# Four pieces of the next rows' preparation at earlier points of VectorE's order, and one tile for the last three row stores

## The chip, the cores and the metric

The kernel runs on one core of a Trainium2 chip. The metric is the device time of one launch in microseconds (us), the median of several runs. TensorE, VectorE, ScalarE and GpSimd each work through a queue of instructions in order; SyncE (SP) issues most of the DMAs. Semaphores tie the queues together. In the profile they are PE, DVE, ACT, POOL and SP.

## The reference

x has 8 rows (batch entries) of 512 tokens with 256 features. All is in float32. What is computed, with the shapes that matter:

```python
nx = layer_norm(x) * ln_gamma + ln_beta                    # (8, 512, 256)
k, v = context @ Wk, context @ Wv                          # context (8, 64, 256)
weights = softmax(nx @ Wq @ k.T / 16)                      # (8, 512, 64)
evidence = weights @ v
combined = concat([nx, evidence, anchor])                  # 768 features, anchor is cond of the row
router = softmax(combined @ router_W + router_b)           # 3 experts
h = silu(combined @ e_w1[e] + e_b1[e])                     # (8, 512, 512) for each expert
routed = sum_e router[e] * (h @ e_w2[e] + e_b2[e])
g = sigmoid(silu(combined @ gate_w1 + gate_b1) @ gate_w2 + gate_b2)
out = x + g * (routed @ out_w + out_b)
```

## The kernel before

**Tiling.** Two rows of x are handled together: a loop runs over four row pairs, j = 0 to 3. For each, `gate_layer` makes the hidden layer of the gate, `expert_layer` is called for the experts e = 0, 1, 2, and `outputs` makes the gate, the experts' second layer and the stores. Products of two rows are combined in a scheme with seven products in place of eight, so that each hidden chunk is put together from several PSUM parts. `keep_part` (L830) is a copy on ScalarE that takes a part out of PSUM and thereby lets TensorE go on in that bank, `add` (L827) is an addition on VectorE, `silu` (L821) is on ScalarE. `weigh` (L868, L872) multiplies hidden chunks by the router's probabilities, on VectorE, from a list that is worked off in order at several points. In `outputs`, `subtract` (L1063) forms differences of hidden chunks ahead of the products that read them, L1073 starts a sum with the biases, and `keep` (L1079) adds to it from PSUM.

**Order.** Every queue's order is the order of the Python calls; no scheduler changes it. The preparation of the next row pair is spread over the work of this one: a dictionary names steps for points such as (1, "B"), point B in the layer of expert 1, and `run` calls the steps of a point in the order in which they were put. Points in a layer are, in order, W, A, B, C and D. Work that belongs to the weights, which are turned and combined while the first row pair runs, is put in the same way and ahead of the next rows' steps. Two of its parts matter here: `transpose_second` (L486, VectorE) turns a block of second-layer weights into the tile scr_w2T, and `second_layer` (L494) multiplies it on TensorE and copies it out on ScalarE (L499). `combine_second` (L233 to L236) then works on GpSimd.

**Preparation of the next pair.** Its steps, with their engines:

- `load_x` (L146, SP) loads the two tiles of x, b0 and b1.
- `statistics` (L540, L541, VectorE) finds mean and variance, four pairs of instructions for a tile.
- `deviation` (L544, ScalarE) takes the square root of the variances. The square root and the silu belong to different function tables of ScalarE.
- `normalize` (L549, L552, VectorE) is one reciprocal and four multiplications in place.
- `store_x` (L600, SP) stores the normalized tile to scratch memory, four DMAs a tile, and `regroup_x` (L468, SP) loads it again in another order, eight DMAs.
- `router_part` (L590, VectorE) multiplies the normalized x by a vector and sums along x, four instructions a tile, each with a second one that reads the sum; `logits` in it has a small memset (L581) on GpSimd.
- `transpose_blocks` (L612, VectorE, then L563 on ScalarE) turns what was regrouped.

`load_x_blocks` (L468, SP) loads this pair's x once more for the final addition (tile xb, read by L1096 on GpSimd).

**The end.** The last pair ends in `outputs` with products by tokens: `token_experts` gives three PSUM tiles, and `finish_rows` (L1179 to L1181) multiplies and adds on VectorE and stores. Its output tile has the tag yb, of which there are two buffers; the tile y_tokens before it has the same tag.

Of the kernel before, what the change touches and what calls it, by code (L numbers as in the profile page):

```python
# [8 lines left out]
F32 = mybir.dt.float32  # L9
# [7 lines left out]
def kernel(  # L17
# [51 lines left out]
    nc = tc.nc  # L69
    P = 128  # L70
    B, T, H = x.shape
# [3 lines left out]
    NT = T // P  # L75
# [15 lines left out]
    work = ctx.enter_context(tc.tile_pool(name="work", bufs=2))  # L91
# [439 lines left out]
    S = {}  # L531
# [376 lines left out]
    def finish_groups(j, groups):  # L908

        for n in groups:  # L910
            silu(j, n, 0, 1, U[n])
            if n:
                add(n, 1, 0, Z[n])
# [5 lines left out]
    def expert_layer(j, e, steps):  # L919
        a, b = PAIRS[e]  # L920

        def run(point):
            for step in steps.get((e, point), ()):
                step()

        if e:
            finish_groups(j, PAIRS[e - 1])
        for i in range(2):
            S["h", i, e] = h_tile(i, e, f"h_{2 * j + i}_{e}")
        U[a] = bank(3, f"ps_u_{j}_{a}")  # L930
        nx_product(j, a, 1, True)
        keep_part(a, 0, 0, U[a])
        if not e:
            nx_product(j, 0, 4)
        U[b] = bank(1, f"ps_u_{j}_{b}")
        nx_product(j, b, 1, True)
        if not e:
            finish_groups(j, (0,))
        keep_part(b, 0, 0, U[b])
        finish_odd(j, PAIRS[e - 1] if e else (0,))  # L940
        if not e:
            silu(j, 0, 1, 1)
        if e > 1 or e and j:
            weigh(j, 4)
            run("W")
            weigh(j, 1)
        spares(*Z_BANKS[1 - e % 2])
        nx_product(j, a, 2)
        add(a, 0, 0, Y[a])
        nx_product(j, a, 5)  # L950
        keep_part(a, 1, 1, Z[a])
        run("A")
        nx_product(j, a, 6)
        keep_part(a, 1, 0, U[a])
        silu(j, a, 0, 0)
        nx_product(j, b, 6)
        keep_part(b, 1, 0, U[b])
        nx_product(j, b, 2)
        add(b, 0, 0, Y[b])
        nx_product(j, b, 5)  # L960
        keep_part(b, 1, 1, Z[b])
        silu(j, b, 0, 0)
        spares(*Z_BANKS[1 - e % 2], 4, 6)
        run("B")
        for n in (a, b):
            nx_product(j, n, 7)
            add(n, 1, 1, U[n])
        for n in (a, b):
            weigh_early(n)
        run("C")  # L970
        if e:
            weigh(j, 6 if j or e > 1 else 10)
        for n in (a, b):
            silu(j, n, 1, 1)
            weigh_rest(n)
        for n in (a, b):
            nx_product(j, n, 3)
        run("D")
        for n in (a, b):
            nx_product(j, n, 4)  # L980
        if e + 1 < E:
            fresh(j, e + 1)
            evidence(j, [(m, False) for m in (a, b)] + [(m, True) for m in PAIRS[e + 1]])
        else:
            evidence(j, [(m, False) for m in (a, b)])
# [13 lines left out]
    def outputs(j, steps):  # L999
# [22 lines left out]
        u, z, y = (bank(i, f"ps_g{n}_{j}") for n, i in (("u", 0), ("z", 2), ("y", 4)))  # L1022
# [89 lines left out]
        def finish_late(r, ps, i, row):  # L1112
            g = gated(ps, i, row, slice(0, T))
            nc.vector.tensor_tensor(r, r, g, ALU.add)
            nc.vector.transpose(g, r)
            store(g, i, row, slice(0, T), (nc.scalar, nc.sync))
# [57 lines left out]
            for q in range(NQ):  # L1174
                product(ps, hidden(j, q, 1, 0)[:, t * P : (t + 1) * P], a(q, 0, 1), start=q == 0)

        def finish_rows(rest, ps, t, queue):
            y = work.tile([P, P], F32, tag="yb", name=f"y_rows_{t}")
            nc.vector.tensor_tensor(y, ps, rest[:, 0, t - 1, :], ALU.mult)  # L1179
            nc.vector.tensor_tensor(y, y, rest[:, 1, t - 1, :], ALU.add)  # L1180
            queue.dma_start(out[2 * j, t * P : (t + 1) * P, :P], y)  # L1181
# [14 lines left out]
        for t in range(1, NT):  # L1196
            token_experts(tokens[t - 1], t)
        finish_late(r21, u, 1, 0)
        for t in range(1, NT):
            finish_rows(rest, tokens[t - 1], t, nc.scalar if t % 2 else nc.sync)  # L1200


    with tc.manual_schedule(engines=None):
# [62 lines left out]
        for j in range(NP):  # L1266


            within, between = {}, {}

            def put(where, n, step, *args):
                where.setdefault(n, []).append(lambda: step(*args))

            if j == 0:
                put(within, "gate", value_weights, 0, 1)
                put(within, (0, "A"), anchor_rows, 1)
                put(within, (0, "A"), router_logits, 0)
                put(within, (0, "A"), load_second, 1)
                put(within, (0, "B"), second_bias)
                put(within, (0, "C"), transpose_second, 0)  # L1280
                put(within, (0, "C"), anchor_columns, 1)
                put(within, (0, "C"), anchor_rows, 2)
                put(within, (0, "C"), router_exp, 0)
                put(within, (0, "D"), router, 0)
                put(within, (0, "C"), load_second, 2)
                put(within, (0, "D"), second_layer, 0)
                put(within, (0, "D"), spread_probabilities, 0)
                put(within, (0, "D"), combine_second, 0)
                put(within, (1, "A"), transpose_second, 1)
                put(within, (1, "B"), second_layer, 1)  # L1290
                put(within, (1, "B"), combine_second, 1)
                put(within, (1, "C"), transpose_second, 2)
                put(within, (1, "C"), anchor_columns, 2)
                put(within, (1, "D"), second_layer, 2)
                put(within, (1, "D"), combine_second, 2)
            if j:
                put(within, "gate end", spread_probabilities, j)
            if j and j + 1 < NP:
                put(within, (0, "B"), statistics, 2 * j + 3, 0, NT)
            put(within, (0, "C" if j == 0 else "B"), value_weights, j, 2)  # L1300
            put(within, (1, "C"), load_x_blocks, 2 * j)
            put(within, (2, "A"), gate_differences, j)
            put(within, (2, "C"), load_x_blocks, 2 * j + 1)
            if j + 1 < NP:
                b0, b1 = 2 * j + 2, 2 * j + 3
                if j == 0:
                    put(within, "gate", load_x, b0)
                    put(within, "gate", load_x, b1)
                if j + 2 < NP:
                    put(between, "begin", load_x, b0 + 2)  # L1310
                    put(between, "begin", load_x, b1 + 2)
                put(within, (0, "A" if j else "D"), statistics, b0, 0, NT)
                if j == 0:
                    put(within, (1, "A"), statistics, b1, 0, NT)
                for i in range(2):
                    put(within, (0, "D") if j else (1, "B"), deviation, j + 1, i)
                for b in (b0, b1):
                    put(within, (1, "W") if j else (1, "C"), normalize, b)
                    put(within, (1, "W") if j else (1, "C"), store_x, b)
                put(within, (1, "C") if j else (1, "D"), regroup_x, b0)  # L1320
                put(within, (1, "A") if j else (2, "C"), router_part, b0)
                put(within, (1, "D") if j else (2, "C"), router_part, b1)
                put(between, "begin", transpose_blocks, b0)
                put(between, "gate", regroup_x, b1)
                put(between, "begin", value_weights, j + 1, E)
                put(between, "begin", store_router_rows, j + 1)
                put(between, "begin", spread_router_rows, j + 1)
                put(between, "P5", transpose_blocks, b1)
                put(between, "P2", scores, j + 1)
                put(between, "P2", combine_x, j + 1, nc.gpsimd)  # L1330
                put(between, "P7", softmax, j + 1)
                put(between, "P7", value_weights, j + 1, 0)
                put(between, "P7", router_logits, j + 1)
                put(between, "P3", value_weights, j + 1, 1)
                put(between, "P3", turn_weights, j + 1)
                put(between, "P3", router_exp, j + 1)
                put(between, "P4", router, j + 1)
            gate_layer(j, within)
            for e in range(E):
                expert_layer(j, e, within)  # L1340
            outputs(j, between)


# [32 lines left out]
```

## Time and profile before

| | us |
|---|---|
| median of 3 runs | 471.18 (471.0 to 471.22) |
| the profiled execution, whole time | 471.0 |
| its span in the profile | 468.9 |
| TensorE busy | 459.8 |
| VectorE busy | 363.7 |
| ScalarE busy | 214.0 |
| GpSimd busy | 97.6 |
| granted TensorE clock | 0.998 of full speed |

The span runs from the first to the last recorded event; 2.1 us of the whole time lie around it. All times of day in the text count from the start of the span. Row pair 0 takes the span from about 25 to 148 us, and each further pair some 106 us. In a line of the timeline the columns are start, duration, engine, line, operation, output and inputs, count, and in brackets the idle time of that engine before it with what ended it. In a line of the chain of waits they are start, duration, and what was running.

### The profile page before, as it was taken

What the parts mean: (1) busy time and instruction counts of PE and PEld (TensorE: products, weight loads), DVE (VectorE), ACT (ScalarE), POOL (GpSimd) and SP (SyncE); (2) the same over time, 40 slices, a digit from 0 to 9 for tenths busy, and PEclk for the clock granted to TensorE, in tenths of its full rate; (3) what the DMA queues carried; (4) which work ended last, traced back from release to release, by engine and by line L of the source; (5) the groups of instructions that cost most, each with busy time, mean ns of one, the idle gap of its engine ahead of it and who ended that gap; (6) DMA issues with size and microseconds to landing.
All of it is one profiled execution on the core that took longest, in us unless ns stands there. A gap on an engine that the chain in (4) does not pass through costs nothing.

```text
span 468.9 us, 4767 instructions
## 1 busy us (share of the span) xinstructions
PE 459.8 (98%) x1473; PEld 209.8 (45%) x1473; DVE 363.7 (78%) x672; ACT 214.0 (46%) x369; POOL 97.6 (21%) x133
## 2 busy tenths in 40 slices
PE   9999999999999999999999999999999999999995
PEld 7544555343444344444444344444444344444454
DVE  3995648999799659879799659879899625788963
ACT  3345666466222576557221576448221446457000
POOL 6547315201072300001072300001072300000020
PEclk9999999999999999999999999999999999999999
DMA  8989933532012405812011414702011570000013
GB/s 274 282 167 159 139 125 89 91 89 46 6 22 37 127 41 125 147 44 45 6 24 26 99 78 100 122 5 46 7 22 22 88 184 0 0 0 1 0 31 59
DMA packets 119352, 34.87 MB, mean 74 GB/s; under 512 B 106060, under 2 KB 116352, under 8 KB 118816
## 3 DMA queue, kind: packets, MB, share of 16 engines
q1 hardware_dynamic: 115168, 26.95, 29.7%
q0 software_dynamic: 2128, 6.78, 4.8%
q10 hardware_dynamic: 2032, 0.85, 0.7%
q8 instruction: 11, 0.18, 0.2%
q14 instruction: 13, 0.11, 0.1%
HBM read 27.17 MB, written 7.39 MB: 74 GB/s over the span
## 4 chain that ended last, share of the span: by engine, by line
PE 70%; DVE 25%; issue 3%; DMA 1%; ACT 0%; DVEq 0%
PE ps_u L788 31%; PE ps_z L788 12%; PE ps_y L788 11%; DVE h L1063 5%; DVE h L872 4%; PE ps_vw L763 3%; PE ps_gu L788 3%; DVE r L1094 2%; DVE yb L1095 2%; DVE r L1093 2%; PE ps_w2o L494 1%; PE ps_gz L788 1%; DVE wT L691 1%; DVE h L868 1%; DVE r L1073 1%
## 5 line engine op out<-in xcount | busy, mean ns | idle before, releaser
L872 DVE TENSOR_TENSOR h<-h,pb 128x512 f32<-128x512 f32 x96 | 62.3, 699 | 6.0 <-ACT h L821 6.0
L788 PE MATMUL ps_u<-h,w2o 128*128 128x512 f32 x144 | 64.1, 594 | 0.0
L788 PE MATMUL ps_u<-nxT,w 128*128 128x512 f32 x112 | 55.9, 608 | 0.8 <-ACT h L830 0.8
L821 ACT ACTIVATE h<-h,abias 128x512 f32<-128x512 f32 x72 | 49.2, 718 | 14.9 <-DVE h L827 14.5
L788 PE MATMUL ps_z<-wT,vw 64*128 64x512 f32 x104 | 49.5, 605 | 0.0
L1096 POOL TENSOR_TENSOR yb<-yb,xb 128x512 f32<-128x512 f32 x14 | 18.4, 1314 | 148.6 <-DVE yb L1095 121.2
L788 PE MATMUL ps_z<-h,w2s 128*128 128x512 f32 x96 | 42.6, 593 | 0.2 <-DVE r L1079 0.2
L830 ACT COPY h<-ps_u 128x512 f32<-128x512 f32 x48 | 27.9, 581 | 30.5 <-PE ps_u L788 30.1
L788 PEld LDWEIGHTS ps_u<-h,w2o 128*128 128x128 f32 x144 | 27.0, 190 | 32.5 <-issue 29.4
L827 DVE TENSOR_TENSOR h<-h,ps_y 128x512 f32<-128x512 f32 x24 | 16.4, 683 | 25.0 <-PE ps_y L788 21.1
L1063 DVE TENSOR_TENSOR h<-h,h 128x1024 f32<-128x1024 f32 x24 | 34.3, 1483 | 0.0
L408 POOL DMA_DIRECT2D vrd<-vw x8 | 5.0, 627 | 140.7 <-ACT vw L770 140.7
L788 PEld LDWEIGHTS ps_u<-nxT,w 128*128 128x128 f32 x112 | 19.8, 189 | 30.9 <-issue 24.2
L821 ACT ACTIVATE h<-ps_u,abias 128x512 f32<-128x512 f32 x24 | 16.5, 687 | 28.5 <-PE ps_z L788 28.2
L827 DVE TENSOR_TENSOR h<-h,ps_z 128x512 f32<-128x512 f32 x24 | 16.1, 684 | 16.8 <-PE ps_z L788 16.7
L788 PE MATMUL ps_u<-wT,vw 64*128 64x512 f32 x56 | 28.1, 617 | 0.6 <-DVE hg L827 0.4
L788 PEld LDWEIGHTS ps_z<-h,w2s 128*128 128x128 f32 x96 | 18.1, 190 | 23.5 <-issue 21.5
L788 PE MATMUL ps_y<-nxT,w 128*128 128x512 f32 x56 | 28.6, 592 | 0.0
L788 PE MATMUL ps_z<-T,ws 128*128 128x512 f32 x56 | 28.6, 592 | 0.0
L788 PE MATMUL ps_y<-wT,vw 64*128 64x512 f32 x56 | 27.0, 596 | 0.0
L763 PE MATMUL ps_vw<-w,vT 128*128 128x512 f32 (+1 forms) x64 | 26.9, 543 | 0.0
L788 PE MATMUL ps_u<-T,ws 128*128 128x512 f32 x56 | 26.7, 594 | 0.0
(241 smaller groups left out, 800.4 us busy)
## 6 DMA issues: line engine op xcount, KB each, us to landing
pb<-pd POOLq DMA_DIRECT2D x4, 1536.0 KB, 7.4
xb<-in_x_dram SPq DMA_DIRECT2D x64, 64.0 KB, 2.4
out_dram<-yb SPq DMA_DIRECT2D x56, 64.0 KB, 2.0
w<-in_L_xcond_e_w_dram SPq DMA_DIRECT2D x6, 512.0 KB, 8.9
x<-in_x_dram SPq DMA_DIRECT2D x24, 128.0 KB, 3.2
xd<-x SPq DMA_DIRECT2D x24, 128.0 KB, 2.3
xg<-xd SPq DMA_DIRECT2D x48, 64.0 KB, 2.4
scr_wa<-in_L_xcond_e_w_dram SPq DMA_DIRECT2D x3, 512.0 KB, 21.8
```

The lines of the kernel that those rows point to most:

```text
L408: nc.gpsimd.dma_start(S["vrd", j][i].rearrange("e c -> c e"), S["vw", j][row_half(i), R0:])
L763: nc.tensor.matmul(ps, vT[:, k, j * 2 * CT : (j + 1) * 2 * CT], w1[:, KH + k, n0:n1], start=(k == 0), stop=(k == KH - 1),)
L788: nc.tensor.matmul(ps, lhsT, rhs, start=start, stop=True, skip_group_check=not start)
L821: nc.scalar.activation(h, h if src is None else src, AF.Silu, bias=abias[:, c, 2 * j + i : 2 * j + i + 1])
L827: nc.vector.tensor_tensor(h, h, part, ALU.add)
L830: nc.scalar.copy(chunk(n, i, d), part)
L872: nc.vector.tensor_tensor(h, h, S["pb", j][:, i, :, 2 * q // RC, :], ALU.mult)
L1063: nc.vector.tensor_tensor(d, p, m, ALU.subtract)
L1093: nc.vector.tensor_tensor(r, r, ps, ALU.add)
L1094: nc.vector.tensor_tensor(r, r, S["hg", row, i], ALU.mult)
L1095: nc.vector.transpose(yb, r)
L1096: nc.gpsimd.tensor_tensor(yb, yb, S["xb", 2 * j + row][:, i, :], ALU.add)
```

## The change

Two things are changed.

In the output stage of the last pair, one tile of three slices is taken ahead of the loop, and `finish_rows` gets its slice, where it took a tile of its own in each pass.

In row pair 0 alone, steps that prepare row pair 1 are put elsewhere. A new point S lies near the head of each `expert_layer`, behind the previous expert's `finish_groups`; only expert 1 of the first pair has steps there. For j = 0:

| step | before | after |
|---|---|---|
| statistics of the second tile | (1, A) | (0, D), behind those of the first |
| square roots, both | (1, B) | (1, S) |
| normalize and store_x, both tiles | (1, C) | (1, S) |
| regroup_x of the first tile | (1, D) | (1, C) |
| router_part, both tiles | (2, C) | (1, B) |

```diff
@@ expert_layer
         if e:
             finish_groups(j, PAIRS[e - 1])
+        run("S")
         for i in range(2):
@@ outputs
-        def finish_rows(rest, ps, t, queue):
-            y = work.tile([P, P], F32, tag="yb", name=f"y_rows_{t}")
+        def finish_rows(y, rest, ps, t, queue):
             nc.vector.tensor_tensor(y, ps, rest[:, 0, t - 1, :], ALU.mult)
             nc.vector.tensor_tensor(y, y, rest[:, 1, t - 1, :], ALU.add)
             queue.dma_start(out[2 * j, t * P : (t + 1) * P, :P], y)
...
         finish_late(r21, u, 1, 0)
+        y = work.tile([P, NT - 1, P], F32, tag="yb", name="y_rows")
         for t in range(1, NT):
-            finish_rows(rest, tokens[t - 1], t, nc.scalar if t % 2 else nc.sync)
+            finish_rows(y[:, t - 1, :], rest, tokens[t - 1], t, nc.scalar if t % 2 else nc.sync)
@@ the list of steps
                 put(within, (0, "A" if j else "D"), statistics, b0, 0, NT)
                 if j == 0:
-                    put(within, (1, "A"), statistics, b1, 0, NT)
+                    put(within, (0, "D"), statistics, b1, 0, NT)
                 for i in range(2):
-                    put(within, (0, "D") if j else (1, "B"), deviation, j + 1, i)
+                    put(within, (0, "D") if j else (1, "S"), deviation, j + 1, i)
                 for b in (b0, b1):
-                    put(within, (1, "W") if j else (1, "C"), normalize, b)
-                    put(within, (1, "W") if j else (1, "C"), store_x, b)
-                put(within, (1, "C") if j else (1, "D"), regroup_x, b0)
-                put(within, (1, "A") if j else (2, "C"), router_part, b0)
-                put(within, (1, "D") if j else (2, "C"), router_part, b1)
+                    put(within, (1, "W" if j else "S"), normalize, b)
+                    put(within, (1, "W" if j else "S"), store_x, b)
+                put(within, (1, "C"), regroup_x, b0)
+                put(within, (1, "A" if j else "B"), router_part, b0)
+                put(within, (1, "D" if j else "B"), router_part, b1)
```

## The prediction

> **What bounds the kernel now.** First the page's busy times, then TensorE's waits, then the chain of waits at the two stalls and at the end.
>
> ```profile
> span 468.9 us, 4767 instructions
> ...
> PE 459.8 (98%) x1473; PEld 209.8 (45%) x1473; DVE 363.7 (78%) x672; ACT 214.0 (46%) x369; POOL 97.6 (21%) x133
> ```
>
> TensorE is idle for 468.9 - 459.8 = 9.1 us in all. A change that leaves TensorE's own work alone, as this one does, can win no more than a part of that. The list of TensorE's waits over the whole span says where it lies:
>
> ```profile
> PE ps_wake L295 <- DVE warm_t L186: 1.1, 1, 1.1
> PE ps_u L788 <- ACT h L830: 0.8, 1, 0.8
> PE ps_u L788 <- DVE h L1063: 0.8, 1, 0.8
> PE ps_u L788 <- DVE hg L827: 0.4, 2, 0.2
> PE ps_z L788 <- DVE r L1079: 0.2, 1, 0.2
> ```
>
> Columns: total us, times, longest. They come to 3.3 us; 1.1 is the start. The same list cut to 40 to 160 us holds just the two waits of 0.8, so both lie in row pair 0. The rest, 5.5 us, is the end: the last matmul ends at about 463.4 (36 token matmuls from 459.18, lasting 4.18).
>
> The chain of waits leads up to the first stall:
>
> ```profile
> 90.29 0.61 DVE h L827
> ...
> 90.92 0.72 ACT h L821
> 91.64 0.48 ACT h L830
> ...
> 92.17 1.12 PE ps_u L788 x2
> ```
>
> VectorE's add is late, ScalarE's silu waits for it, the copy behind the silu frees PSUM, and TensorE waits for the copy. VectorE itself waited for nothing. Its timeline shows that it is idle early in this row pair, then busy without a gap from 72.84 to 124.97:
>
> ```profile
> 57.99 0.69 DVE L827 TENSOR_TENSOR h<-h,ps_z 128x512 f32<-128x512 f32 x1 [3.85 <-PE ps_z L788]
> ...
> 63.37 0.69 DVE L827 TENSOR_TENSOR h<-h,ps_y 128x512 f32<-128x512 f32 x1 [3.84 <-PE ps_y L788]
> ...
> 71.91 0.69 DVE L827 TENSOR_TENSOR h<-h,ps_u 128x512 f32<-128x512 f32 x1 [3.93 <-PE ps_u L788]
> ...
> 74.94 1.38 DVE L552 TENSOR_SCALAR x<-x,mv,rstd 128x256 f32<-128x256 f32 x4
> ```
>
> The brackets are idle time: 3.85 + 3.84 + 3.93 = 11.6 us before the queue fills up. So both stalls are a VectorE backlog. At the end, the chain of waits:
>
> ```profile
> 462.18 0.05 DVE y_rows L1179
> 462.22 2.83 DMA out_dram<-y_rows
> ...
> 465.14 0.30 DVE y_rows L1179
> ```
>
> The third last-row tile waits 2.35 us for the store of the first to leave its buffer.
>
> **What the Trainium skill says.** "ScalarE: Activation LUTs", What ACT_TABLE_LOAD costs, gives 1.28 us for a table load plus a drain of 1.38, 2.66 in all. The trace agrees on the load alone: the next function starts within 0.02 us.
>
> ```profile
> 71.65 1.28 ACT L544 ACT_TABLE_LOAD   x1
> 72.95 0.48 ACT L544 ACTIVATE sd<-mv,eps_t 128x4 f32<-128x4 f32 x2
> 73.45 1.28 ACT L821 ACT_TABLE_LOAD   x1
> ```
>
> I take 1.28 and keep 2.66 for the range. "SBUF — State Buffer", Who interferes with whom: VectorE and GpSimd shut each other out when a VectorE instruction has two SBUF inputs or uses both ports. The trace agrees: GpSimd's L233 on 128x256 takes 2.63 us at 78.78, beside VectorE's weightings, against 0.73 at 71.71; three weightings (L872) take 3.48 there. "DMA: Bandwidth & Descriptors", Anatomy of one DMA, has about 2.0 us of fixed cost; the row stores here land after 1.6 to 2.8.
>
> **The change, part by part.** No instruction is added or removed except that three small tiles become one; the rest moves.
>
> *Statistics of the second next row (L540, L541)*: from 65.20 to 67.30, 2.1 us, to behind those of the first, which end at 54.14. They then run to 56.2, inside the idle time that ends at 57.99. Their x was issued by 44.5 and lands 3.3 later. Cost nothing; without that idle time it would be 2.1 us.
>
> *Square roots (L544)*: ScalarE would run them after the two silus that end at 59.50: load to 60.8, roots to 61.3. Copies follow at 61.59 and 62.45, as now, since the trace has copies (L770 at 50.01) between an exponential and the next load without a load of their own. Then the silu load, 63.03 to 64.3, and the queue behind it: two silus to 65.7, copies to 66.7, a silu, copies of the other group to 68.4, a silu to 69.0. TensorE needs those copies when it accumulates again at 70.85; the w2o copy at 69.32 is on time. So the 2.56 us of loads are hidden, with 2 us to spare.
>
> *Normalizations (L549, L552)*: 1.5 us each (74.73 to 76.23, to 77.74), 3.0 in all. Now they wait for the roots: 61.35 to 64.35. Behind them on VectorE is the add for ps_y, ready at 63.37, so 1.0 late; it ends at 65.0. The transposes of the next second-layer weights (L486, 1.3 us) then end at 66.3. TensorE reads these at 67.39: 1.1 us to spare. The silu waiting for the add is behind the table load anyway.
>
> *Sums along x (L590)*: eight pairs of 0.42 and 0.08, 95.25 to 98.87, 3.6 us. They go behind the second add of ps_y (ready at 66.7, so 66.8 to 67.4) and end at 71.1, before the add at 71.91. Spare 0.8. GpSimd has nothing between 60.1 and 71.71, so neither part meets it.
>
> *DMAs and queues*: SP's eight stores (L600, 3.72 us at 76.34) go to 62.9 to 66.6. The eight xb loads that SP issued at 53.09 (4.21 us) are now behind them; GpSimd first uses xb at 129.87, so nothing. The eight regrouping loads (81.15, 4.40 us) end near 75.3 instead of 85.5, for transposes at 105.60: nothing. The loads of the next x, at 97.11 because L590 held them, come near 80; nobody waits. The pb load (issued at 56.61, 7.5 to land) may share a microsecond of DMA with the stores; it is used at about 75. GpSimd's 0.10 us memset of lg moves behind its work ending at 74.6.
>
> *What that does to the stalls*: from 74.8 VectorE has 3.0 us less ahead of it. Ten weightings and differences, 8.4 us at present, end near 83 instead of 86.1; the add that ended at 90.81 then follows a silu of ScalarE and ends near 88. ScalarE's copy for TensorE is done at 89.6, needed at 91.35: the first stall goes, **-0.81**. Without the 3.6 us of sums, VectorE then catches up and waits for TensorE. In the output stage the last gate add starts with TensorE, at 104.0 - 0.8 = 103.2 to 103.9, two transposes follow to 105.1, nine weightings (5.6 us as at 106.82 to 112.44) to 110.7, four L1073 (2.7) to 113.4, the add L1079 to 114.0 and the first L1063 (1.15) to 115.2. TensorE wants it at 116.15 - 0.81 = 115.3. Next late would be this same L1063, with just 0.1 to spare: I take **-0.81** and keep 0 for the range.
>
> *The end*: with one tile for the three rows no row waits for another's store. The third starts when TensorE is done, 463.38 + 0.14 (the lag of the second row, 462.04 to 462.18) = 463.52 instead of 465.14: **-1.62**. Its store then follows the others more closely; those had 2.4 and 2.8 against 1.6 to land. Transfers are nearly over by 465, so I take no loss; the range has 0.6 of it.
>
> **Sum**: -0.81 - 0.81 - 1.62 = -3.24. The profiled execution took 471.0 (span 468.9), so 467.8; the median of the runs, 471.18, is 0.18 above it, so 467.9.
>
> **The rivals.**
> *A, the early stage is too tight (chance 0.18).* If roots came 1.4 later (the skill's drain), VectorE would pass on to the transposes 0.3 late and to the next 0.6 late, and the stall at L1063 could stay. For it: 0.1 and 0.8 us of room. Against: the trace's loads. That leaves the end plus 0 to 0.8: -1.6 to -2.4, 468.7 to 469.6.
> *B, the last store takes up the gain (0.06).* If landing takes 2.8 as the first row's, the end gives 0.4 and the sum is -2.0: 469.2. Against: the DMA share falls to nothing at 465.
> *C, slower: a slice counts as the whole tile (0.03).* Then row two waits for row one's store (465.05), is stored at 465.8, lands 2.4 later, and row three is stored near 468.9 instead of 465.8: +3.1, net +1.5, 472.7. It decides if any write to a part must wait for the reader of another part. Against: SP issued a load into one half of scr_w2T at 48.83, while VectorE, earlier in program order, was only starting to write the other half (48.86 to 50.16); and lg was written by VectorE and by GpSimd's memset at the same 23.00. For it: no slice of a y tile is seen so far.
> *Nothing happens* is excluded for the end, where the buffer wait is plain; it would need A and B together, 0.02.
>
> **How the numbers follow.** Main case 0.69: 467.9, from 467.1 (0.2 of it from the small waits of 0.4 and 0.2 in the list, the rest from a last store that lands in 1.0 instead of 1.6 once the others are gone) to 468.5 (half of L1063's wait left and 0.2 at the end). With A and B the range goes to 469.6. A measurement can tell about 0.2%, 0.9 us, from no change; main, A and B are beyond it (0.93, of which 0.01 for their lowest ends goes to no change). Same 0.03; slower 0.05, C and 0.02 for an ordering that I have not seen.
>
> **What would show it.** Right: TensorE's list of waits holds neither L830 nor L1063 in row pair 0; VectorE's L552 lies near 61 to 64 and L590 near 67 to 71, with idle time between 83 and 104; no y_rows waits for another row's store, TensorE ends near 461.8 and the last add near 462.5 (465.76 now). Wrong: a wait of TensorE on L486 near 67 or 74, a wait on L1063 of over 0.2, or stores that land after 2.8 us.

## The result, and the profile after

The changed kernel takes 467.5 us (median of 5 runs, 467.23 to 467.62) against 471.14 before (471.0 to 471.22): the ratio is 0.9921, with a 95% interval of 0.991 to 0.9933. That is 3.6 us less, 0.4 below the time that was predicted. The profiled execution took 467.23 us, its span is 465.2. Lines behind the new point S have moved on by one, so L1063 of before is L1064 here.

The page's busy times:

```profile
span 465.2 us, 4763 instructions
...
PE 459.4 (99%) x1473; PEld 210.0 (45%) x1473; DVE 363.8 (78%) x672; ACT 214.2 (46%) x369; POOL 95.8 (21%) x133
```

TensorE is idle for 5.8 us instead of 9.1, and its own work is the same to 0.4 us. The list of TensorE's waits over the whole span (total us, times, longest):

```profile
PE ps_wake L295 <- DVE warm_t L186: 1.1, 1, 1.1
PE ps_u L788 <- DVE hg L827: 0.4, 2, 0.2
PE ps_rb L381 <- POOL scr_small L278: 0.2, 1, 0.2
PE ps_z L788 <- DVE r L1080: 0.2, 1, 0.2
```

Both waits of 0.8 are gone, and from 40 to 160 us the list is empty. VectorE's timeline of the changed kernel shows how the work has spread:

```profile
58.01 0.69 DVE L827 TENSOR_TENSOR h<-h,ps_z 128x512 f32<-128x512 f32 x1 [0.70 <-PE ps_z L788]
...
61.15 0.18 DVE L549 RECIPROCAL rstd<-sd 128x4 f32<-128x4 f32 x1 [1.60 <-ACT sd L544]
...
66.82 0.69 DVE L827 TENSOR_TENSOR h<-h,ps_y 128x512 f32<-128x512 f32 x1 [0.76 <-PE ps_y L788]
...
71.92 0.69 DVE L827 TENSOR_TENSOR h<-h,ps_u 128x512 f32<-128x512 f32 x1 [0.80 <-PE ps_u L788]
...
100.45 0.69 DVE L1017 TENSOR_TENSOR hg<-g_r,ps_gy 128x512 f32<-128x512 f32 x1 [2.12 <-PE ps_gy L788]
102.17 0.69 DVE L1017 TENSOR_TENSOR hg<-g_r,ps_gz 128x512 f32<-128x512 f32 x1 [1.03 <-PE ps_gz L788]
```

The three early gaps of 3.85, 3.84 and 3.93 us have shrunk to 0.70, 1.60 + 0.76 and 0.80. At 100 us, where VectorE used to be behind, it now waits for TensorE. ScalarE's timeline has the roots at their new place:

```profile
59.53 1.28 ACT L544 ACT_TABLE_LOAD   x1
60.82 0.48 ACT L544 ACTIVATE sd<-mv,eps_t 128x4 f32<-128x4 f32 x2
61.60 0.59 ACT L830 COPY h<-ps_u 128x512 f32<-128x512 f32 x1 [0.29 <-PE ps_u L788]
62.46 0.59 ACT L830 COPY h<-ps_u 128x512 f32<-128x512 f32 x1 [0.27 <-PE ps_u L788]
63.06 1.28 ACT L821 ACT_TABLE_LOAD   x1
```

The copies between the roots and the next silu need no load of their own, and both came as soon as TensorE had the part ready. TensorE's timeline at the two places, first before:

```profile
90.33 1.02 PE L788 MATMUL ps_u<-nxT,w 128*128 128x512 f32 x2
92.17 1.12 PE L788 MATMUL ps_u<-nxT,w 128*128 128x512 f32 x2 [0.81 <-ACT h L830]
...
98.63 1.12 PE L788 MATMUL ps_gu<-hg,gw_sb 128*128 128x512 f32 x2
...
110.84 5.31 PE L788 MATMUL ps_z<-h,w2s 128*128 128x512 f32 x12
116.97 5.42 PE L788 MATMUL ps_u<-h,w2s 128*128 128x512 f32 x12 [0.81 <-DVE h L1063]
```

and after:

```profile
90.34 1.88 PE L788 MATMUL ps_u<-nxT,w 128*128 128x512 f32 x4
...
97.50 1.13 PE L788 MATMUL ps_gu<-hg,gw_sb 128*128 128x512 f32 x2
...
103.71 5.31 PE L788 MATMUL ps_u<-h,w2o 128*128 128x512 f32 x12
108.86 1.02 PE L788 MATMUL ps_gu<-g_t,gw_sb 128*128 128x512 f32 x2
109.72 5.31 PE L788 MATMUL ps_z<-h,w2s 128*128 128x512 f32 x12
115.01 5.42 PE L788 MATMUL ps_u<-h,w2s 128*128 128x512 f32 x12
```

Four matmuls follow each other at 90.34 where before two stood at 90.33 and two at 92.17. The gate's first matmul starts at 97.50 instead of 98.63, 1.13 earlier; the product behind L1064 at 115.01 instead of 116.97, 1.96 earlier. The second place is not quite free, though the list of waits is empty there: the twelve matmuls from 109.72 take 5.29 us until the next start, where the twelve from 103.71 take 5.15. TensorE's weight load at 115.01 still waited for L1064, and 0.14 us stays lost. At the end, TensorE's last matmuls and the rows in VectorE's timeline:

```profile
457.19 4.18 PE L788 MATMUL ps_tokens<-w2o,h 128*128 128x128 f32 x36
...
459.58 0.29 DVE L1179 TENSOR_TENSOR y_rows<-ps_tokens,rest 128x128 f32<-128x128 f32 x1 [0.47 <-DMA out_dram<-y_tokens]
...
461.41 0.29 DVE L1179 TENSOR_TENSOR y_rows<-ps_tokens,rest 128x128 f32<-128x128 f32 x1 [0.69 <-PE ps_tokens L788]
```

The third row waits for TensorE, whose token matmuls end at 457.19 + 4.18 = 461.37, and no longer for a store. It starts 3.73 us earlier than before (465.14): 1.99 is what TensorE brings along from row pair 0 (459.18 to 457.19), and 1.74 is the end's own. The span is 3.7 shorter, so the last store took less than 0.1 back.

### The profile page after: what moved, and what is told of

The parts are those of the page before. It is cut to its first block, busy times and chain, and to the rows that moved or that the text cites. A ratio compares the mean times of both kernels' runs of the same rounds, so it can differ in the third digit from the quotient of the medians.

```text
span 465.2 us, 4763 instructions
## 1 busy us (share of the span) xinstructions
PE 459.4 (99%) x1473; PEld 210.0 (45%) x1473; DVE 363.8 (78%) x672; ACT 214.2 (46%) x369; POOL 95.8 (21%) x133
## 4 chain that ended last, share of the span: by engine, by line
PE 74%; DVE 19%; issue 3%; DMA 2%; POOL 0%; DVEq 0%; POOLq 0%
PE ps_u L788 34%; PE ps_z L788 14%; PE ps_y L788 12%; DVE h L1064 5%; PE ps_vw L763 3%; PE ps_gu L788 3%; PE ps_w2o L494 2%; DVE r L1095 2%; DVE yb L1096 2%; DVE r L1094 2%; PE ps_gz L788 1%; DMA scr_small<-in_L_xcond_router_W_dram 1%; DVE wT L691 1%; DMA scr_small<-in_L_xcond_e_b_dram 1%; DVE pv L701 1%
## 5 line engine op out<-in xcount | busy, mean ns | idle before, releaser
L830 ACT COPY h<-ps_u 128x512 f32<-128x512 f32 x48 | 28.0, 583 | 28.6 <-PE ps_u L788 26.2
L1064 DVE TENSOR_TENSOR h<-h,h 128x1024 f32<-128x1024 f32 x24 | 34.3, 1482 | 0.0
```

The source lines that it names most:

```text
L830: nc.scalar.copy(chunk(n, i, d), part)
L1064: nc.vector.tensor_tensor(d, p, m, ALU.subtract)
```

## The experiments

The theory has two parts. **Backlog**: VectorE's work for row pair 1 stood in a stretch where VectorE was behind, and the idle time before it can hold that work. **Buffer reuse**: the third last row waited for a store only because it had to have the first row's buffer. The rivals are that one part does it all or that they share their gain, that the early stretch is too tight, that the stores take up the gain at the end, and that it is the move of the sums that counts. Differences of spans are the finer measure here. A span in the text is that of one profiled execution, but TensorE's start times in row pair 0 repeat within some 0.4 us, while the intervals of the timed ratios are about 0.6 us to either side. And the time that lies outside of the span, which a median holds too, is not the same in every kernel: 2.2 us in the kernel before, 1.8 with the one tile alone, 1.9 with the moves alone, 2.0 in the changed kernel, in each within 0.1 over all its runs. Why it differs is not known.

### The one tile alone

```diff
-        def finish_rows(rest, ps, t, queue):
-            y = work.tile([P, P], F32, tag="yb", name=f"y_rows_{t}")
+        def finish_rows(y, rest, ps, t, queue):
...
+        y = work.tile([P, NT - 1, P], F32, tag="yb", name="y_rows")
```

> The kernel before with the last change alone: one tile of three slices for the last rows. Buffer theory (the third row's 2.35 us wait for the first row's store is the whole of it, and TensorE's end takes over as what it waits for): 1.7 us faster, 469.4, with TensorE's two waits of 0.8 in row pair 0 still there. Rival (the stores take up the gain, since they follow each other more closely): 0.6 us or less.

Measured: 469.06 us against 471.29 (ratio 0.9952, 0.9938 to 0.9965); span 467.3, 1.6 less than before. From VectorE's timeline:

```profile
463.53 0.29 DVE L1178 TENSOR_TENSOR y_rows<-ps_tokens,rest 128x128 f32<-128x128 f32 x1 [0.68 <-PE ps_tokens L788]
```

TensorE's two waits of 0.8 are still in its list. The time is 2.2 below before, more than the 1.7 expected, which lies within the interval (1.6 to 2.9); the span says 1.6, and 0.4 of the other 0.6 lies outside of it. The rival that the stores take the gain is out.

### The moves alone

The changed kernel with `finish_rows` as it was before.

> The four moved pieces of row pair 0 alone, with a tile for each last row as before. Backlog theory: both waits of TensorE go and the row pair ends 2.0 us earlier, 469.2; the third last row still waits about 2.3 us for the first one's store. Together with the run of the tile alone it gives the whole 3.6 to 3.7. Rival (the two parts share one gain, or one needs the other): the two parts' gains do not add up to that.

Measured: 469.06 us against 471.29 (0.9952, 0.9939 to 0.9964); span 466.9, 2.0 less than before. TensorE's waits in row pair 0 are gone, and the third row waits as it did:

```profile
463.19 0.29 DVE L1180 TENSOR_TENSOR y_rows<-ps_tokens,rest 128x128 f32<-128x128 f32 x1 [2.40 <-DMA out_dram<-y_rows]
```

The spans of the two halves add up: 1.6 + 2.0 = 3.6, and the whole change has 3.7. The medians of the times add up to 4.5, against 3.6 for the whole. That surplus comes from outside of the spans: the medians of all runs' spans are 1.8 and 1.9 shorter, 3.7 together. As far as the spans can tell, the two parts are independent.

### Rows with buffers of their own

```diff
-            y = work.tile([P, P], F32, tag="yb", name=f"y_rows_{t}")
+            y = work.tile([P, P], F32, tag=f"yr{t}", name=f"y_rows_{t}", bufs=1)
```

> The kernel before with three separate tiles for the last rows, each with a buffer of its own, so that none waits for the store of another or of y_tokens; row pair 0 as before. Buffer theory: it is the reuse and not the single tile that counts, so the same as with one tile: a span of 467.3, 1.6 shorter than before, the third row starting within 0.15 us of TensorE's end; that the first row no longer waits for the store of y_tokens brings nothing, since TensorE sets the third. Rival (what counts is that the rows lie in one tile): no gain, 471.2.

Measured: 469.07 us against 471.06 (0.9959, 0.9946 to 0.9973); span 467.4. VectorE's timeline:

```profile
461.26 0.25 DVE L1179 TENSOR_TENSOR y_rows<-ps_tokens,rest 128x128 f32<-128x128 f32 x1
...
463.64 0.29 DVE L1179 TENSOR_TENSOR y_rows<-ps_tokens,rest 128x128 f32<-128x128 f32 x1 [0.72 <-PE ps_tokens L788]
```

The first row no longer waits for y_tokens, the third starts where TensorE (459.42 + 4.18 = 463.60) lets it, and the gain is the one of the single tile. It is the reuse that cost the time, not the shape of the tile; and the earlier start of the first row brings nothing.

### The sums back in their old place

```diff
-                put(within, (1, "A" if j else "B"), router_part, b0)
-                put(within, (1, "D" if j else "B"), router_part, b1)
+                put(within, (1, "A") if j else (2, "C"), router_part, b0)
+                put(within, (1, "D") if j else (2, "C"), router_part, b1)
```

> The changed kernel with the sums along x (L590) back in the layer of expert 2. Backlog theory: VectorE is idle for 2.12 + 1.03 + 0.18 = 3.3 us between 98.3 and 103.0 in the changed kernel, the sums take 3.7, so only some 0.4 of them reaches the output stage, of which 0.1 is spare: 0.2 to 0.4 us slower than the changed kernel, 467.7 to 467.9. Rival (the move of the sums is what removes the second wait): the wait of 0.8 on L1063 is back, 468.3.

Measured: 467.31 us against 471.29 (0.9917, 0.9903 to 0.993); span 465.1. That is the changed kernel's time; neither 0.2 to 0.4 nor 0.8 was lost. In VectorE's timeline the sums stand at 92.79 to 96.48 again, and then:

```profile
101.34 0.68 DVE L1017 TENSOR_TENSOR hg<-g_r,ps_gy 128x512 f32<-128x512 f32 x1
102.03 0.69 DVE L1017 TENSOR_TENSOR hg<-g_r,ps_gz 128x512 f32<-128x512 f32 x1
102.90 0.69 DVE L1017 TENSOR_TENSOR hg<-g_r,ps_gu 128x512 f32<-128x512 f32 x1 [0.18 <-PE ps_gu L788]
```

The first gate add is late, the second just on time, and the third waits for TensorE again. VectorE has caught up with 0.18 to spare. The expectation had counted 3.3 us of idle time against 3.7 of sums. The sums take 3.61 (92.79 to 96.40), one gap of 0.17 at 97.65 had been left out, and VectorE's instructions start 0.60 us apart when nothing holds them up (99.54 to 100.14), less than the 0.68 that each lasts. So the fourth move, that of the sums, is worth nothing that these runs can show once the normalization has moved.

### The kernel before without the sums

```diff
+    def no_sums(j):
+        nc.gpsimd.memset(logits(j)[:, 2, :], 0.0)
...
+                    put(within, (2, "C"), no_sums, 1)
```

It stands in row pair 0 in place of the two `router_part` calls for the next rows.

> The kernel before without the sums along x for row pair 1 (they are left out, and a memset stands in for them; so the router of that pair lacks a term); the normalization stays where it was. Backlog theory: the first wait of TensorE, at the copy of expert 2, comes before the sums and stays, costing about 1.1; VectorE then catches up, so the second goes: 0.8 faster than before, 470.3. Rival (the normalization's place is behind both waits): no change, 471.1, with both waits.

Measured: 469.03 us against 471.29 (0.9952, 0.9939 to 0.9964); span 467.3. TensorE's waits:

```profile
PE ps_u L791 <- ACT h L833: 0.8, 1, 0.8
```

The first wait stays and the one on the subtraction is gone, as expected, and the product behind it starts at 116.28, 0.7 to 0.8 earlier than in kernels that have the wait (116.97 and 117.08). But the median is 2.3 us lower in place of 0.8. The span is 1.6 shorter: TensorE's last 36 matmuls start 0.74 earlier (459.18 to 458.44); the third row, which waited 1.12 instead of 2.35 for the first row's store, gains a further 0.51 (465.14 to 463.89 in all); and the span ends 0.36 sooner after it. Another 0.4 lies outside of the span, 1.8 us here against 2.2.

### The same, with the one tile, and once more

The first has the sums left out as above and the one tile for the rows; the second is the same kernel as the last.

> The kernel before with the one tile for the last rows and without the sums along x for row pair 1 (left out, with a memset in their place). The run without the sums gained 2.2 us where TensorE's own times showed 0.8; its last rows ended 0.45 early and its span 0.35 after that. Theory (the rest came from the end, where the third row waited 1.1 instead of 2.35 us for a store that landed sooner): with one tile there is no such wait to shorten, so 0.8 faster than the one tile alone, a span of 466.5 and about 468.3. Rival (leaving out the sums does more for TensorE than the trace shows): 2.2 faster than the one tile alone, 466.9.

> The kernel before without the sums along x for row pair 1, a second time. Theory: TensorE's times in row pair 0 repeat (0.8 earlier behind L1063), and the third row's wait again depends on how soon the store of y_tokens lands (1.6 or 2.3 us): if it takes 2.3 again, the wait is 1.1 again and the time near 469.0; if it takes 1.6, the wait is 2.3 and the time 470.3. Rival (chance of one execution): the profile shows 1.6 and 2.3 while the timed runs are at 469.0 again.

Measured: with the one tile 467.99 us against 471.06 (0.9935, 0.9922 to 0.9947), span 466.2; once more without it 469.05 (0.9958, 0.9946 to 0.9971), span 467.3. With the one tile, leaving the sums out is worth 1.1 (469.06 to 467.99, and in the spans), close to the 0.8 of the theory and far from the rival's 2.2; the third row starts 0.81 earlier (463.53 to 462.72). In spans, the first run had gained 0.5 more than that, 1.6, as much as its third row gained beyond TensorE. VectorE's timeline of the second:

```profile
461.60 0.29 DVE L1182 TENSOR_TENSOR y_rows<-ps_tokens,rest 128x128 f32<-128x128 f32 x1 [1.36 <-DMA out_dram<-y_tokens]
...
463.90 0.29 DVE L1182 TENSOR_TENSOR y_rows<-ps_tokens,rest 128x128 f32<-128x128 f32 x1 [1.08 <-DMA out_dram<-y_rows]
```

It repeats. The store of y_tokens landed after 2.3 to 2.5 us in all three executions without the sums, and after 1.6 in the traces before and after; the first row came later by about as much, its own store then went out 1.8 to 2.0 us instead of 1.1 after the four stores of transposed blocks, and landed in 1.6 instead of 2.8. So a store that came late seems to have made the next one quick; no run varies that alone.

The DMA records show what very likely made y_tokens late. In all three executions a packet of the queue that the profile calls "instruction" starts near 460.0 us, while this store's packets are moving, and takes 0.57 to 0.64 us. The store's last nine packets start within 0.01 us of its end, some 0.5 us after the others. In every kernel that has the sums, the last packet of that queue comes at the very end of the span, after all the stores. So leaving the sums out did more than shorten VectorE's work: it also took this packet away from the end. The span ends 3.4 us after the third row's start in the kernels without the sums, and 3.7 to 3.8 in the others that are compared here. That the packet is the reason for both was not tested.

### How much room the early stretch has

Three versions of the changed kernel make the normalization later:

```diff
-                    put(within, (0, "D"), statistics, b1, 0, NT)
+                    put(within, (1, "S"), statistics, b1, 0, NT)
```

> The changed kernel with the statistics of the second tile at the new point S, ahead of the square roots, in place of the end of expert 0. Spare-time theory: VectorE takes 2.1 us for them from 59.5, the roots run at 61.7 instead of 60.8, the normalization ends near 65.2, the transposes L486 near 67.1, just in time for TensorE at 67.4, and the rest has caught up at 71.9: no change against the changed kernel, 467.5. Rival (the early stage is too tight): the transposes or the next ones come late and TensorE waits on L486, 0.5 to 1 us slower.

```diff
+                if j == 0:
+                    put(within, (1, "S"), load_table, AF.Exp)
                 for i in range(2):
                     put(within, (0, "D") if j else (1, "S"), deviation, j + 1, i)
```

> The changed kernel with one more table load and a one-column activation ahead of the square roots, so that these come 1.5 us later. Spare-time theory: 1.1 us are spare at the first transposes and 0.8 at the adds of 71.9, and VectorE is idle for 0.76 + 0.80 in between, so it is all but absorbed: 0 to 0.2 slower than the changed kernel, 467.5 to 467.7, with any wait of TensorE on L486. Rival (the early stage is too tight): 0.6 or more, and the wait on L1064 back.

```diff
                     put(within, (1, "S"), load_table, AF.Exp)
+                    put(within, (1, "S"), load_table, AF.Sigmoid)
```

> The same with two more table loads and activations, so that the roots come 3.0 us later. Spare-time theory: now ScalarE's first copy (L830) ends near 64.9 where TensorE wants it at 64.0, about 1.0 us of wait, and the sums end near 73.5, 0.6 later than the adds behind them, so the second-layer weights (L486 near 74) cost 0.6: 1.4 to 1.8 slower than the changed kernel, 468.9 to 469.3. Rival (VectorE has 11.6 us of idle time early on, of which the change uses 8.7, so that almost 3 us are left): 0.3 or less.

Measured: the late statistics 467.4 us (0.9922, 0.991 to 0.9935), one load more 467.28 (0.992, 0.9907 to 0.9934), two loads more 468.95 (0.9955, 0.9942 to 0.9967), all against 471.06. The first two are the changed kernel's time. With one load more, VectorE's timeline shows the room all but used up:

```profile
62.75 0.18 DVE L549 RECIPROCAL rstd<-sd 128x4 f32<-128x4 f32 x1 [3.12 <-ACT sd L544]
...
72.00 0.69 DVE L827 TENSOR_TENSOR h<-h,ps_u 128x512 f32<-128x512 f32 x1 [0.15 <-PE ps_u L788]
```

Of 0.76 and 0.80 us of idle time, 0.15 are left, and TensorE has lost nothing. With two loads more, TensorE's timeline:

```profile
64.88 1.95 PE L788 MATMUL ps_u<-T,ws 128*128 128x512 f32 x4 [0.81 <-ACT h L830]
...
68.47 3.88 PE L494 MATMUL ps_w2o<-ow_sb,scr_w2T 128*128 128x256 f32 x16
...
75.62 3.80 PE L494 MATMUL ps_w2o<-ow_sb,scr_w2T 128*128 128x256 f32 x16
```

The first wait is at the copy behind the late roots, where it was expected. The weights' matmuls come 1.06 later (67.41 to 68.47) and the next ones 1.33 later (74.29 to 75.62); so of the second cost, expected at 0.6 near 74, just 0.27 showed, and it was lost in the matmuls from 68.47, whose transposes (L486) ran until 69.01. In all 1.5 us were lost against the changed kernel, 1.4 in the span. The rival that almost 3 us of VectorE's idle time are left, so that nothing is lost, is out: most of the loss came over ScalarE's copy, and VectorE's idle time lay ahead of the late roots (4.63 us at 64.11), where it could not help what came behind them. What counts is the idle time ahead of the instruction that TensorE waits for next.

### The last store from another queue

```diff
-            finish_rows(y[:, t - 1, :], rest, tokens[t - 1], t, nc.scalar if t % 2 else nc.sync)
+            finish_rows(y[:, t - 1, :], rest, tokens[t - 1], t, nc.sync if t % 2 else nc.scalar)
```

> The changed kernel with the queues of the last three row stores swapped: the first and third from SP, the second from ScalarE. An issue takes 0.36 us on either queue in the changed kernel's trace, and the third is the last work of all: no change, 467.5 within 0.2. Rival (ScalarE's queue holds the last store back behind its earlier ones): up to 0.4 faster, 467.1, the best version so far.

Measured: 467.06 us against 471.06 (0.9921, 0.9907 to 0.9934); span 465.3, where the changed kernel has 465.2. The median is lower by 0.4, as the rival had it, but its five runs reach from 466.82 to 468.37, the ratio is the changed kernel's, and the third row starts 0.04 after TensorE's end as it did there. There is no difference that this measurement can show. None of the experiments beat the changed kernel.

## Why the prediction was right, point by point

**What bounds the kernel**: right. Of the 3.7 us of the span, 3.3 came out of TensorE's idle time, 9.1 us before and 5.8 now, and by TensorE's start times the two waits and the end hold all of it.

**Statistics**: right that they are hidden. They ended at 57.31 instead of the predicted 56.2. They followed those of the first tile without a gap, but VectorE's whole queue was 0.95 us later there (the first tile's began at 52.86, before at 51.91), since it had waited 1.25 us for a DMA (tile vr) at 43.23; 0.70 of idle time was left. Placed some 4.6 us later still, at 59.70, they cost nothing either.

**Square roots**: right. Predicted at 60.8 to 61.3, they ran at 60.82 to 61.30. The Trainium skill, "ScalarE: Activation LUTs", What ACT_TABLE_LOAD costs, has a drain of 1.38 us with each load; here again the roots start 0.01 us after the load's 1.28, and roots that came 1.5 us later cost nothing. So a delay of the drain's size would not have made rival A come true; twice that delay does cost time, and mostly at a place that the rival's text had not named, the copy L830.

**Normalizations and what is queued behind**: right. Predicted 61.35 to 64.35, they ran at 61.15 to 64.25; the add behind them ended at 64.84 (65.0), the transposes at 66.06 (66.3).

**Sums**: their place is right (67.42 to 71.12; 71.1 was predicted), their part in the sum is not. The working had VectorE catch up "without the 3.6 us of sums". It catches up with them in their old place too. Either 3 us of the normalization or 3.6 us of sums taken out of the stretch is enough to free TensorE from the wait on L1063: the moves without that of the sums do it (sums back: nothing lost), and so does leaving the sums out (no sums: that wait gone). The wait on L830 comes before the sums and is removed by the other moves. Of these it is VectorE's part that counts: ScalarE, whose table loads moved as well, had in the kernel before sat idle for 1.92 us ahead of the silu at 90.92, waiting for VectorE's add.

**DMAs**: right in that none mattered. SP's stores took until 68.0 rather than 66.6, and the regrouping ended at 77.3 rather than 75.3; its reader comes at 103.65.

**The stalls, -0.81 and -0.81**: right that both waits go, and the first by the predicted chain: VectorE's add ended at 87.92 (88) and ScalarE's copy at 89.65 (89.6). What they bring was put too low: 1.13 and 0.83, 1.96 in all. The term that was mis-sized is the first. The trace shows 0.81 us of idle time ahead of the matmuls at 92.17, but the step from 90.33 to 92.17 took 1.84 where a pair takes 0.86 (0.98 more), the pair after the wait took 0.96 until the next (0.10 more), and a further 0.05 was lost at 94.85.

The idle time of a wait in this view is less than what the wait costs. It counts from the shown end of the matmuls before it: a pair is shown with 1.02, but the next one starts 0.86 after it where nothing holds it up, 0.16 ahead of that end. The same holds for the second wait, where twelve matmuls took 6.13 until the next start instead of 5.15: it too cost 0.98 in its step.

Of this second 0.98, about 0.84 were won and 0.14 are left. The 0.1 that L1064 was to have to spare was not there: the prediction had taken the moment at which TensorE wants it from the shown end (116.15), too late by the same 0.16, and TensorE came earlier still by what the first wait brought beyond 0.81. The first third of L1064 starts at 113.75 and takes 1.22; TensorE goes on at 115.01, where it would have at 114.87. That the second term came out so close to 0.81 is luck: a larger cost and a rest that stays make up for each other.

**The end, -1.62**: 1.74. The mechanism was right. The third row starts 0.04 after TensorE's end and not 0.14 as the second row did before. The last store did not take up the gain (rival B): it landed in 1.6 us. Slices of one tile did not wait for each other (rival C): the third slice was written at 461.41, while the second one's store, issued at 460.75 and landing 2.5 later, was under way. The row stores ran from 1.6 with the queues drained to 2.8 behind four others.

**The sum**: -3.24 was predicted for the profiled execution, and its span shrank by 3.7: 0.34 more from the stalls and 0.12 more from the end make up the difference.

## What to carry to other kernels

Where an engine that others wait for has no idle time ahead of the wait, look upstream in its queue for idle time, and move into it whatever is ready by then; check for each gap which instruction ends it and who waits for that one, as room in one gap is no room in the next. One move may be enough: put the others back one at a time before all are kept. Read what a wait costs from the start times of TensorE's instructions, as its idle time is less. For the last tiles of a kernel, count the buffers of their tag: a tile that has to wait there for a store to land adds that wait to the end (2.35 us here, of which 1.74 could be won).

## What the runs showed of the hardware that was not expected

Three waits of TensorE that the traces put at 0.81 us each (two before, one with two loads more) cost 0.98 in their step. A 64 KB store of a row landed in 1.6 us when its queues had drained and in 2.8 right behind four stores of transposed blocks; in the kernels without the sums a store that landed 0.8 us late went with a next one that landed 1.2 us sooner, and its own last packets had started only after an instruction packet of 0.57 to 0.64 us.
